# The boundary between images: x in 128 + 64 channels, a convolution by halves of rows, and a new order of the chains

## The chip, the cores and the metric

The kernel runs on one core of one Trainium2 chip. The metric is the device time of one execution in microseconds, the median of three runs. Everything is float32. The five engines are named as the profile names them: PE (TensorE matmul) with PEld (its weight loads), DVE (VectorE), ACT (ScalarE), POOL (GpSimd) and SP (SyncE, which here issues the transfers).

## The reference

Eight images of 64 x 64 tokens with 192 channels pass through two layers, each `x + layer(groupnorm(x))`. Layer 0 is a state-space block with an MLP; the change doesn't touch it. Layer 1 is a scan of each image in four directions (16 states, 384 inner channels). Cut to what matters here:

```python
x = x + _L1_conv_ref(_gn(x), ...)

xz = einsum('bhwc,dc->bhwd', x, in_proj_w)          # 192 -> 2 x 384
xc, z = split(xz, 2, axis=-1)
xc = silu(conv3x3_depthwise(xc) + conv_b)           # 384 channels, 64 x 64
xs = stack of xc by rows, by columns, and both reversed
x_dbl = einsum('bkdl,kcd->bkcl', xs, x_proj_weight) # dt (12), B (16), C (16)
delta = softplus(dts @ dt_projs_weight + bias)
h = exp(delta * A) * h + delta * u * B;  y = sum over n of C * h
y = sum of the four directions (brought back to row order) + xs * Ds
y = (y - mean(y)) * rsqrt(var(y) + 1e-5) * ln_gamma + ln_beta   # over 384
return (y * silu(z)) @ out_proj_w                   # 384 -> 192
```

## The kernel before

Layer 0 runs first over all images and leaves them in eight DRAM tensors `x1s[b]` of 192 channels by 4096 tokens. Layer 1 (`layer1`) then treats one image after another. For each `b` it builds a boundary and then the scan stage.

The scan stage (`main` in `scan`) goes through 32 steps (4 directions, 8 chunks of 512 tokens) of 24 units: two scans on DVE (`run`, L1662), a product with C on POOL (L1676), decays and weighted B on ACT (L1620, L1605), transposes and sums over states on PE (L1646, L1691). Its order is that of the program.

The boundary consists of generators ("chains") whose order `Flow` makes up when the kernel is built: `Flow.run` keeps a planned time for each engine, and takes again and again the chain whose next step can start first, with its rank times 0.01 us added (a chain given later ranks later). Each step names its engine and a planned duration. The order so found is kept on each engine's queue as it is[...].

The chains of `front` prepare image `b`, on tiles of 96 channels by two for the 192 of x:
- `load` (L1133) reads x in tiles of 512 tokens, three times over, once for each block of 128 of the 384 inner channels (`d`);
- `project` (L1148) makes `p_x` with two matmuls over 96 channels each;
- `fill` (L1178) copies it with a bias to a padded image `pad` (66 x 66; two of them);
- `convolve` waits for the whole `pad`: tap 0 on ACT (L1199), eight more on DVE (L1209), each over 4096 tokens;
- `store` and `by_tokens` apply silu (L1222) and store `xo` in three layouts: as it is (L1227), with rows and columns exchanged (`xt`, L1237 and L1241), and by tokens, by way of PE transposes (L1256), copies `xq` on ACT (L1265) and transfers of 256 KB from two buffers (L1268).

The chains of `finish` end image `b - 1`, whose sum `yacc` lies in SBUF: `centre` (mean by matmul, L1288; subtraction, L1296), `square` (L1306), `norm` (L1324, L1325, then the scaling L1331 on DVE and gamma and beta on ACT, L1338), `gate` and `silu` (p_z, L1368, and z, L1386), `product` (L1398), and `project` (p_o, L1415, two matmul groups of 96 output channels; L1424 adds x; L1427 stores). All go by tiles of 512 tokens.

The chain `prologue` starts once all of `front` is stored (`"front"`): it frees front's SBUF space, opens the pools of the scan stage there, loads the first chunk `xc` (L1469), and makes the first `p_d` (L1488), `p_dt` (L1523), `de` (L1536), `duT` (L1552), ten `pw` and two decays. The scan stage's first scan follows once the boundary's work on DVE is through. The last boundary has only `finish`, the first only `front` and the prologue.

The scaled weights (`scaled`, L1107) are made from `wi`, which stays in SBUF for all of layer 1. One PSUM bank (`m1`) belongs to layer 1 as a whole; the boundary has seven, five for `"mm"` and two for `"fx"`.

Of the kernel before, what the change touches and what calls it, by code (L numbers as in the profile page):

```python
# [28 lines left out]
NB1 = TT // 128  # L29
NP1 = N // 2  # L30
# [6 lines left out]
BIG = 60.0  # L37

# [57 lines left out]
class Flow:  # L96
# [48 lines left out]
    def start(self, req, ready):  # L145

        if req[0] == "wait":
            return (-1.0, max(ready, self.at[req[1]])) if req[1] in self.at else None
        if req[0] == "take":
            return (-1.0, max(ready, min(self.slots[req[1]]))) if self.slots[req[1]] else None  # L150
        engine, _, _, after, table = req
        t = max(ready if after is None else after, self.free[engine])
        if engine == "ACT" and table and table != self.table:
            return t + self.TABLE + self.STAY, t + self.TABLE
        return t, t

    def run(self):
        while self.chains:
# [8 lines left out]
            if req[0] == "take":  # L167
# [866 lines left out]
def layer1(tc, consts, x1s, mv1, out, w_in, w_x, w_dt, w_out):  # L1034
# [7 lines left out]
    with ExitStack() as ctx:  # L1042
        pool = lambda name, bufs, **kw: ctx.enter_context(tc.tile_pool(name=name, bufs=bufs, **kw))
        wp = pool("w1", 1)
        sp = pool("s1", 1)
        mp = pool("m1", 1, space=PSUM)
# [5 lines left out]
        wi = wp.tile([CP, CT, 2 * DIN], F32, name="wi1")  # L1052
# [25 lines left out]

        sc, sh = gn_affine(tc, sp, mp, mv1.rearrange("p b t s -> p (b t) s"), grp, eps)
        pb = mp.tile([128, TT], F32, name="p_gb", tag="mm")  # L1080
# [10 lines left out]
        nc.vector.tensor_copy(gb.rearrange("p m b -> p (m b)"), pb[:, : 2 * DT * nb])  # L1091
        keeper = []
# [7 lines left out]
        def scaled(w, b, half):  # L1100

            for ct in range(CT):
                r = yield step(
                    "ACT",
                    0.6,
                    lambda: [
                        nc.scalar.activation(  # L1107
                            w[:, ct],
                            wi[:, ct, half * DIN : half * DIN + DIN],
                            AF.Copy,  # L1110
                            scale=sc[:, b * CT + ct : b * CT + ct + 1],
                        )
                    ],
                )
            return r

        def front(f, cx, mq, b, xo):
# [3 lines left out]
            wx_b = fp.tile([CP, CT, DIN], F32, name="wx1b")  # L1121
            pads = [fp.tile([128, HI + 2, WI + 2], F32, name=f"pad{i}") for i in range(2)]
            for tag, n in (("xl", 2), ("fx", 2), ("pad", 2), ("xs", 2), ("xt", 1), ("xq", 2)):
                f.pool(tag, n)
            got = {}

            def load():
                for d in range(DT):
                    for t in range(NT):
                        tk = slice(t * TT, t * TT + TT)  # L1130
                        yield "take", "xl"
                        xl = got["xl", d, t] = fp.tile([CP, CT, TT], F32, name="xl1", bufs=2)
                        r = yield step("SP", 0.1, lambda: [nc.sync.dma_start(out=xl, in_=image(x1s[b])[:, :, tk])])  # L1133
                        f.at["xl", d, t] = r + 3

            def project():
                yield from scaled(wx_b, b, 0)
                for d in range(DT):
                    for t in range(NT):
                        yield "wait", ("xl", d, t)  # L1140
                        xl = got["xl", d, t]
                        yield "take", "fx"
                        ps = got["ps", d, t] = mq.tile([128, TT], F32, name="p_x1", tag="fx", bufs=2)
                        r = f.at["ps", d, t] = yield step(
                            "PE",
                            1.9,
                            lambda: [
                                nc.tensor.matmul(  # L1148
                                    ps, wx_b[:, ct, d * 128 : d * 128 + 128], xl[:, ct], start=ct == 0, stop=ct == 1
                                )  # L1150
                                for ct in range(CT)
                            ],
                        )
                        f.give("xl", r)

            def fill():
# [11 lines left out]
                for d in range(DT):  # L1168
                    yield "take", "pad"
                    pad = pads[d % 2]  # L1170
                    for t in range(NT):
                        yield "wait", ("ps", d, t)
                        ps = got["ps", d, t]
                        r = yield step(
                            "ACT",
                            0.65,
                            lambda: [
                                nc.scalar.activation(  # L1178
                                    pad[:, 1 + t * RT : 1 + t * RT + RT, 1 : WI + 1],
                                    ps.rearrange("p (h w) -> p h w", w=WI),  # L1180
                                    AF.Identity,
                                    bias=gb[:, d, b : b + 1],
# [3 lines left out]
                        f.give("fx", r)  # L1186
                    f.at["pad", d] = r

            def convolve():
                for d in range(DT):  # L1190
                    yield "wait", ("pad", d)
                    yield "take", "xs"
                    xs = got["xs", d] = fp.tile([128, HI, WI], F32, name="xs1", bufs=2)
                    tap = lambda j: pads[d % 2][:, j // 3 : j // 3 + HI, j % 3 : j % 3 + WI]
                    r = yield step(
                        "ACT",
                        3.7,
                        lambda: [
                            nc.scalar.activation(  # L1199
                                xs, tap(0), AF.Identity, bias=v["kb"][:, d : d + 1], scale=kw[:, d, 0:1]  # L1200
                            )
                        ],
                    )
                    for j in range(1, 9):
                        r = yield step(
                            "DVE",
                            4.4,
                            lambda: [
                                nc.vector.scalar_tensor_tensor(xs, tap(j), kw[:, d, j : j + 1], xs, ALU.mult, ALU.add)  # L1209
                            ],  # L1210
                            r - f.LAG,
                        )
                    f.give("pad", r)
                    f.at["conv", d] = r

            def store():
                for d in range(DT):
                    yield "wait", ("conv", d)
                    xs = got["xs", d]
                    for h in range(2):  # L1220
                        half = xs[:, h * HI // 2 : h * HI // 2 + HI // 2]
                        r = yield step("ACT", 1.9, lambda: [nc.scalar.activation(half, half, AF.Silu)], None, "silu")  # L1222
                        r = yield step(
# [5 lines left out]
                                    in_=half.rearrange("p h w -> p (h w)"),  # L1229
# [3 lines left out]
                        )  # L1233
                        f.fork(by_tokens(d, h, xs, r))
                    yield "take", "xt"
                    xt = fp.tile([128, WI, HI], F32, name="xt1")
# [696 lines left out]
```

## Time and profile before

| what | value |
|---|---|
| median of three runs | 23170.1 us (23146.54 to 23176.63) |
| profiled execution, its time / its span | 23175.73 / 23174.0 us |
| busy PE / DVE / ACT / POOL | 94% / 91% / 87% / 70% of the span |
| granted TensorE clock, mean | 0.971 |
| scan stages, first scan to end of last scan | 2027 to 2031 us, eight times |
| between the last scan of an image and the first of the next | 252.1 to 253.7 us, seven times |

A row of a group gives the line, the engine, the operation, the tile written and those read, the shapes and the count; then the busy time in us and the mean ns of one; then the engine's idle time just before, with what released it. A row of a time line gives the start in us, the time from the first start to the last end, and the operations merged into it, in brackets the idle time before them. A row of the chain of waits gives the start, the length and the piece. The median of the runs lies 5.6 us under the profiled execution.

### The profile page before, as it was taken

To read this page: it belongs to the slowest core of one execution; us is meant where nothing else is said; L and a number is where in the kernel's file an instruction comes from. 1 tells how busy PE (TensorE), PEld (TensorE's weight loads), DVE (VectorE), ACT (ScalarE), POOL (GpSimd) and SP (SyncE) were. 2 spreads that over 40 slices of the span, in tenths; PEclk is the share of its full clock that TensorE was granted. 3 is DMA by queue.
4 is the path that set the end of the run, shared out by engine and by line. 5 is a ranking of instruction groups with operands and counts; after the bars stand their busy time and mean duration, and the time that the engine had idled before them with its cause. 6 is when DMAs were issued, how large, how long until landed. Compare 5 with 4: busy or idle time off the path is not lost.

```text
span 23174.0 us, 348545 instructions
## 1 busy us (share of the span) xinstructions
PE 21762.7 (94%) x118788; PEld 11070.5 (48%) x118788; DVE 21110.3 (91%) x22093; ACT 20048.9 (87%) x35418; POOL 16109.5 (70%) x12872
## 2 busy tenths in 40 slices
PE   8999999979998999899999999999999999999999
PEld 4444444435554555455545544554455445544554
DVE  7888888869998999899989998999899989998998
ACT  5666666759997999799979997999899989988998
POOL 1111111139995999599959995999599869976997
PEclk8999999989999999999999999999999999999999
DMA  1111111133333333333333334333433343333332
GB/s 52 45 44 41 45 45 45 42 96 92 95 93 111 92 92 94 111 94 93 90 114 93 92 87 117 95 92 88 117 92 92 89 117 93 93 91 113 92 94 75
DMA packets 1738653, 1998.38 MB, mean 86 GB/s; under 512 B 537280, under 2 KB 1034848, under 8 KB 1727648
## 3 DMA queue, kind: packets, MB, share of 16 engines
q1 hardware_dynamic: 1736864, 1976.07, 31.9%
q8 instruction: 934, 15.30, 0.3%
q14 instruction: 855, 7.00, 0.1%
HBM read 1360.20 MB, written 212.60 MB: 68 GB/s over the span
## 4 chain that ended last, share of the span: by engine, by line
PE 48%; ACT 22%; DVE 11%; POOL 8%; issue 6%; DMA 3%; SPq 2%; DVEq 0%; POOLq 0%; ACTq 0%
PE g L1646 10%; PE y L1691 10%; ACT ea L1620 10%; ACT pw L1605 9%; POOL hs L1676 7%; DVE hs L1662 3%; PE g L1634 3%; PE p_f L957 3%; DVE xs L1209 3%; PE p_d L1488 2%; PE p_x L450 2%; PE p_f L977 2%; PE p_dt L1523 2%; DMA dr<-de 2%; PE p_o L874 2%
## 5 line engine op out<-in xcount | busy, mean ns | idle before, releaser
L1676 POOL TENSOR_TENSOR hs<-hs,cb 128x1024 f32<-128x1024 f32 x6144 | 14584.3, 2374 | 496.4 <-POOL cy L1674 4.2
L1662 DVE TENSOR_TENSOR_SCAN hs<-ea,cy,g 128x512 f32<-128x512 f32 x10752 | 12894.9, 1258 | 187.2 <-PE g L1646 178.1
L1620 ACT ACTIVATE ea<-dr,an 128x512 f32<-128x512 f32 x12288 | 8139.8, 710 | 528.5 <-DVE hs L1662 507.0
L1605 ACT ACTIVATE pw<-duT,bt 128x384 f32<-128x384 f32 x14336 | 7832.7, 600 | 23.5 <-DVE duT L1552 23.5
L1691 PE MATMUL y<-hs,sel 128*64 128x512 f32 x24576 | 6635.2, 618 | 360.0 <-POOL hs L1676 338.6
L1646 PE MATMUL g<-ident,pw 128*128 128x128 f32 x43008 | 6089.9, 281 | 41.1 <-ACT pw L1605 4.8
L1646 PEld LDWEIGHTS g<-ident,pw 128*128 128x128 f32 x43008 | 4612.5, 141 | 2522.6 <-issue 1254.9
L1674 POOL COPY cy<-hs 128x2 f32<-128x2 f32 x6144 | 1160.7, 189 | 2262.0 <-DVE hs L1662 2228.8
L1634 PEld LDWEIGHTS g<-dg,duT 128*64 128x64 f32 x24576 | 1557.4, 136 | 2053.0 <-issue 1484.6
L1634 PE MATMUL g<-dg,duT 128*64 128x128 f32 x24576 | 2257.9, 282 | 169.4 <-DVE hs L1662 106.1
L1691 PEld LDWEIGHTS y<-hs,sel 128*64 128x64 f32 x24576 | 1234.2, 135 | 1563.0 <-issue 865.6
L1662 DVE TENSOR_TENSOR_SCAN hs<-ea,g 128x512 f32<-128x512 f32 x1536 | 1751.8, 1197 | 129.1 <-PE g L1646 116.8
L367 POOL TENSOR_TENSOR s<-xs 96x512 f32<-96x512 f32 x64 | 121.7, 1902 | 2139.6 <-DVE xs L345 1850.2
L1523 PE MATMUL p_dt<-xdbl,wd 13*128 13x512 f32 x1536 | 857.5, 639 | 96.2 <-DVE duT L1552 71.0
L1209 DVE SCALAR_TENSOR_TENSOR xs<-pad,p,xs 128x4096 f32<-128x4096 f32 x192 | 860.9, 4484 | 50.7 <-ACT xs L1199 43.5
L367 POOL TENSOR_TENSOR s<-sq 96x512 f32<-96x512 f32 x128 | 180.1, 1407 | 942.7 <-ACT sq L380 864.4
L1488 PE MATMUL p_d<-xc,wx 128*44 128x512 f32 x1536 | 788.6, 596 | 19.9 <-DMA xc<-xo 19.9
L957 PE MATMUL p_f<-h,wf 96*128 96x512 f32 x1536 | 762.4, 635 | 44.1 <-ACT zs L552 27.5
L345 DVE SCALAR_TENSOR_TENSOR x<-xx,p,x 96x512 f32<-96x512 f32 x1024 | 784.8, 816 | 15.2 <-ACT x L334 15.0
L345 DVE SCALAR_TENSOR_TENSOR xs<-xin,p,xs 96x512 f32<-96x512 f32 x1024 | 746.1, 768 | 3.6 <-ACT xs L334 3.6
L977 PE MATMUL p_f<-m,wf 128*96 128x512 f32 x1536 | 696.1, 604 | 0.0
L1545 PEld LDWEIGHTS p_du<-ident,de 128*128 128x128 f32 x3072 | 323.9, 141 | 610.1 <-DVE de L1536 406.3
(205 smaller groups left out, 19972.1 us busy)
## 6 DMA issues: line engine op xcount, KB each, us to landing
cb<-cd SPq DMA_DIRECT2D x4096, 128.0 KB
dr<-de SPq DMA_DIRECT2D x3072, 128.0 KB
xc<-xo SPq DMA_DIRECT2D x256, 768.0 KB
dg<-dz SPq DMA_DIRECT2D x256, 512.0 KB
e<-csd SPq DMA_DIRECT2D x256, 384.0 KB
xl<-x SPq DMA_DIRECT2D x256, 384.0 KB
ut<-xo SPq DMA_DIRECT2D x128, 768.0 KB
ut<-xo SPq DMA_DIRECT2D x256, 384.0 KB
```

The source lines that it names most:

```text
L345: nc.vector.scalar_tensor_tensor(im(out[:, ct]), tap(ct, j), w[:, ct, j : j + 1], im(out[:, ct]), ALU.mult, ALU.add)
L957: nc.tensor.matmul(ps, wf1[:, ct, mt * 128 : mt * 128 + 128], h[:, ct], start=ct == 0, stop=ct == 1)
L1209: nc.vector.scalar_tensor_tensor(xs, tap(j), kw[:, d, j : j + 1], xs, ALU.mult, ALU.add)
L1488: nc.tensor.matmul(st["p_d"][:44], wx[:, d, k], st["xc"][:, d], start=d == 0, stop=d == DT - 1)
L1523: nc.tensor.matmul(ps, st["wd"][32:45, d * 128 : d * 128 + 128], xds[s % 2][32:45], start=True, stop=True)
L1605: nc.scalar.activation(st["pw", p, j][:, :, i], st["duT"][:, j].rearrange("p (g c) -> p g c", c=64), AF.Copy, scale=st["bt"][:, j, n : n + 1],
L1620: nc.scalar.activation(ea[:, f], state[s]["dr", d][:, f], AF.Exp, scale=an[:, k, p, at : at + 1])
L1634: nc.tensor.matmul(gs[f][i * 64 : i * 64 + 64, j * 128 : j * 128 + 128], state[s]["duT"][:, j, (2 * d + f) * 64 : (2 * d + f) * 64 + 64], ...
L1646: nc.tensor.transpose(gs[f][:, j * 128 : j * 128 + 128], state[s]["pw", p, j][:, 2 * d + f].rearrange("p a b -> p (a b)"), ident,)
L1662: nc.vector.tensor_tensor_scan(rev(h[:, f]), rev(ea[:, f]), rev(g[f]), 0.0 if first(s) else state[s - 1]["cy"][:, p, d, f : f + 1], ALU.mu ...
L1676: o(nc.gpsimd.tensor_mul(h, h, bc(st["cb", p], 1, [128, 2, TT])))
L1691: o(nc.tensor.matmul(y[half[f]], sel, hc[:, f], start=p == ORDER[0] and k > 0, stop=p == ORDER[-1]))
```

## The change

- **x in 128 + 64 channels.** x is read in pairs of tiles: `xa` has channels 0 to 127 of both tiles, `xb` the other 64, those of the first tile on partitions 0 to 63 and those of the second on 64 to 127. `from_pair` makes both tiles' p_x or p_z with four matmuls. `front` reads an image once and holds it for all three blocks. The output projection writes 128 channels of each tile, and the last 64 of both to the two halves of one bank (`p_o2`).
- **Weights.** `scaled` reads its half of the weights from DRAM for each image and scales it in place; `wi` lies in `yacc`'s space and is used once. The scales are brought to the new partitions by four small transfers at the start of the layer.
- **Convolution by halves.** Each `pad` is convolved in two halves of 32 rows, the first once three of the four pairs are filled (`begin`: tap 0; `convolve`: the others). silu, stores and transposes follow by halves; `xq` holds 1024 tokens, and its transfer 512 KB.
- **Normalisation.** gamma goes into the scaling, which becomes three operations per tile on DVE; beta goes into the product, an operation per pair and block. The ACT operations of L1338 go.
- **Prologue.** x, pads and weights are in one pool (`fr1`), the rest of front in another (`fq1`). Once the last half is convolved and the first halves are stored (`"seed"`), the space of the first is freed and the prologue goes up to `bt` and `duT` there; only pools `pw1`, `bc1` and `e1` wait for `"front"`.
- **Order.** Chains have ranks by name (`RANKS`), those of `finish` grow by 8 per pair (`drift`), and `finish` is listed ahead of `front`. The subtraction, the scaling and the output addition are forked off. PSUM is one pool of eight banks in the boundary; `m1` is opened in `main`.

```diff
+RANKS = dict(
+    begin=-31, fill=-131, enter=-89, load=-44, store=-81, convolve=-1, prologue=-61, project=-11, product=-20, norm=-22,
+    square=-24, silu=-131, centre=-36, gate=-94, weights=285, drift=8,
+)
...
+        def pair_of(xa, xb, src, g, out=False):
+            tk = slice(g * GT, g * GT + GT)
+            moves = [(xa, src[:C1, tk].rearrange("p (i l) -> p i l", i=2))]
+            for i in range(2):
+                at = g * GT + i * TT
+                moves.append((xb[i * C2 : i * C2 + C2], src[C1:, at : at + TT]))
...
+        def from_pair(ps, wa, wb, xa, xb, m):
+            return [nc.tensor.matmul(ps[i], wa[:, m], xa[:, i], start=True, stop=False) for i in range(2)] + [
+                nc.tensor.matmul(
+                    ps[i], wb[i * C2 : i * C2 + C2, m], xb[i * C2 : i * C2 + C2], start=False, stop=True
+                )
+                for i in range(2)
+            ]
...
+            def begin():
+                for d in range(DT):
+                    for h in range(2):
+                        yield "wait", ("pad", d, 2 if h == 0 else 3)
...
             def convolve():
                 for d in range(DT):
-                    yield "wait", ("pad", d)
...
-                    for j in range(1, 9):
-                        r = yield step(
-                            "DVE",
-                            4.4,
...
+                    for h in range(2):
+                        yield "wait", ("begun", d, h)
+                        xs, r = got["xs", d, h], f.at["begun", d, h]
+                        for j in range(1, 9):
+                            r = yield step(
+                                "DVE",
+                                2.24,
...
+            def scale(t, yv, rs, r):
+                for d in range(DT):
...
+                            nc.vector.scalar_tensor_tensor(
+                                yv[:, d], yv[:, d], v["gam"][:, d : d + 1], rs, ALU.mult, ALU.mult
+                            )
...
+                                nc.vector.scalar_tensor_tensor(yv, yv, v["bet"][:, d : d + 1], z, ALU.add, ALU.mult)
...
+                            lambda: [
+                                nc.tensor.matmul(
+                                    ps[i * C2 : i * C2 + C2],
+                                    wo[:, d, C1:],
+                                    yacc[:, d, tk(2 * g + i)],
+                                    start=d == 0,
+                                    stop=d == DT - 1,
+                                )
+                                for d in range(DT)
+                                for i in range(2)
+                            ],
...
-            def prologue(f, mq, front_pools):
-                yield "wait", "front"
-                front_pools.close()
-                for name, n in (("pr1", 2), ("dr1", 4), ("pw1", 8), ("bc1", 3), ("e1", 3)):
+            def prologue(f, mq, cx_b, cx_a):
+                yield "wait", ("conv", DT - 1, 1)
+                yield "wait", "seed"
+                cx_b.close()
+                for name, n in (("pr1", 2), ("dr1", 4)):
...
+                yield "wait", "front"
+                cx_a.close()
+                for name, n in (("pw1", 8), ("bc1", 3), ("e1", 3)):
+                    spool(name, n)
```

## The prediction

> **What bounds it now.** I read the busy slices first, then windows cut at the boundaries between images, then the time lines of VectorE and TensorE in one boundary, then the groups.
>
> The scans of L1662 split the span. Layer 0 ends near 4816 us. Each of the eight images then has a scan stage of some 2030 us, with a boundary before it, and a last boundary closes the run. The change leaves the scan stage alone but for the pool that one PSUM bank comes from, so I price the boundaries. Between the scans of two images:
>
> ```profile
> 4816.00:5023.00 207.00, 108.59 (x259) 52.11 (x259) 116.87 (x50) 89.96 (x86) 3.07 (x8) 0.64 0.52 166
> 13900.00:14153.00 253.00, 215.02 (x531) 92.29 (x532) 165.84 (x77) 152.47 (x166) 6.33 (x9) 0.88 0.47 148
> 23034.00:23174.00 140.00, 129.75 (x300) 53.06 (x300) 55.15 (x44) 64.09 (x79) 5.61 (x5) 0.97 0.16 45
> ```
>
> The columns are window and length, busy time of PE, PEld, DVE, ACT and POOL, granted clock, DMA share, GB/s. The first row is the boundary ahead of image 0, the second that between images 3 and 4 (all seven inner ones are 252 to 254), the third the end. An inner boundary keeps PE busy 215 of 252.6 us and DVE 166. Neither is full, so the order inside decides:
>
> ```profile
> 13951.03 36.21 DVE L1209 SCALAR_TENSOR_TENSOR xs<-pad,p,xs 128x4096 f32<-128x4096 f32 x8 [1.14 <-ACT xs L1199]
> ...
> 14033.45 36.12 DVE L1209 SCALAR_TENSOR_TENSOR xs<-pad,p,xs 128x4096 f32<-128x4096 f32 x8
> ...
> 14100.33 6.12 DMA xc<-xo
> ...
> 14138.50 13.54 PE p_o L1415 x24
> ...
> 14152.67 2.32 DVE L1662 TENSOR_TENSOR_SCAN hs<-ea,g 128x512 f32<-128x512 f32 x2
> ```
>
> (Start, length; the transfer and p_o are from the chain of waits, the rest from VectorE's time line.) The last scan ended at 13900.1. The convolution starts 51 us later, since its first 128 channels need all eight p_x tiles and PE alternates them with the means of the previous image. It runs 118.5 us, 108 of them its own. The tail is 83 us: 31 until all stores have left and xc may be loaded, 6 for that load, 20 to du, 5 for the first pw, and 20 in which PE still projects the previous image. So 252.6 = 51 + 118.5 + 83.
>
> **TensorE.** A matmul with 512 columns shows as two entries, 0.43 us apart at full clock (four p_x entries take 1.72). Now p_x, p_z, p_o and the two means have 96 entries each per inner boundary, 384 x 0.43 = 165 us. Afterwards a pair of tiles takes two matmuls over 128 channels and two over 64, the latter on rows 0-63 and 64-127. If these two run side by side, that is 6 entries in time for 8: p_x and p_z fall to 72 each. p_o has two outputs of 128 columns and one bank in halves of 64: also 72. Means stay at 96. That is 312 x 0.43 = 134 us, 31 less.
>
> Side by side? The trace has column halves (y of L1691 starts its two halves 7 ns apart) and one case of row groups:
>
> ```profile
> 14114.05 0.23 PE L1510 MATMUL p_b<-ident,xdbl 16*128 16x16 f32 x1
> 14114.06 0.69 PE L1523 MATMUL p_dt<-xdbl,wd 13*128 13x512 f32 x1
> ```
>
> p_b reads partitions 0-15, p_dt 32-44, and p_dt starts while p_b runs. I take full overlap; the other end is none, 0.86 us more for each of 24 pairs (21 us).
>
> **A rule against it:** the Trainium skill (TensorEngine Tiling (Array Packing), Key Properties) says that changing the tiling mode drains the array. The row: the p_z before that p_b started at 14113.526, its 0.43 ended at 14113.953, p_b began at 14114.047: 0.09 us lost, and as much from p_dt back to p_o. Two switches per pair are 0.18 x 28 = 5 us. A rule without a price would make the gain uncertain; the row leaves 26 us of it. With transposes (96 x 0.11) and the prologue's matmuls PE's work is some 156 us at full clock, against 182 now.
>
> **VectorE** gets more work. L1209 takes 4.484 us for 4096 elements, and the same operation (L499) 0.739 for 512:
>
> ```profile
> L1209 DVE SCALAR_TENSOR_TENSOR xs<-pad,p,xs 128x4096 f32<-128x4096 f32 x192 | 860.9, 4484 | 50.7 <-ACT xs L1199 43.5
> L499 DVE SCALAR_TENSOR_TENSOR cv<-cin,p,cv 128x512 f32<-128x512 f32 x576 | 406.0, 739 | 10.0 <-ACT cv L484 9.8
> L1338 ACT ACTIVATE yacc<-yacc,p 128x512 f32<-128x512 f32 x192 | 149.8, 804 | 38.5 <-DVE yacc L1331 38.5
> ```
>
> That is 1.045 ns per element, so a half of 2048 takes 0.739 + 1.60 = 2.34, and 2.37 with the 0.03 between dependent ones (now 4.513 start to start). 48 x 2.37 = 114 against 24 x 4.513 = 108: +6. The scale by rs becomes 24 short operations (0.66 to 0.74) for 8 of 1.67: +4. The product becomes 12 of 1.19 to 1.27 for 8 of 1.67: +1.5. Output adds are 12 for 16 of 0.61: -2.5. DVE goes from 166 to about 175 us. ScalarE loses L1338 (24 x 0.8 = 19 us per boundary), and with two pairs of token tiles per half also most of its 20 us of waiting for xo<-xq, since the halves lie 19 us apart. It is at 134 us and hides behind DVE; so do SP's issues (12 loads of x for 24, but 24 of the previous image's loads and stores for 16, and six of weights in place of copies of wi: 2 more in all, at 0.35 us). Without that cover a pair of tiles costs its 1.1 us of issue. The new wait for the weights has nothing behind it on ScalarE before 13913, when the first square starts; p_x waits with it.
>
> **The new inner boundary.** PE is free from the scans at 13907.6. SP's first load leaves now at 13905.3, held by the space of the scan's tiles. Four pairs of three transfers at 0.35 us are out by 13910, and 768 KB take up to 6 us (the xc row). PE then needs three p_x pairs (8.3 us) and two means (5.2): 13921. Two fills (0.69) and tap 0 of a half (1.9) follow: the convolution starts near 13924.5, in 24.5 us for 51. This is where most comes from: three of four pairs now suffice, and p_x ranks ahead of the means.
>
> Of the previous image's DVE work (53 us), 5 is done by then. By the ranks, scale, product and output of the last pair and the output of the third stand behind the convolution (drift 8 per pair), about 12 us. The other 36 lies between the taps: 13924.5 + 114 + 36 = 14075.
>
> The tail: the load of xc goes out with the last tap, since what it reads was stored one half (19 us) earlier. Boundary 0 has this chain undisturbed: load at 4997.4, first scan at 5023.2, 25.8 us. The first pw sits where xs, xt and xq lay, so it waits for their last stores: silu with its table load, xt and four copies take 9 us, then 3 MB at the 237 GB/s that the end of this boundary shows, 13 us. This costs between 0 and 9 us on the chain; I take 5, so 31. The 12 us of DVE work and its matmuls lie inside. 14075 + 31 = 14106, with 2 us of gaps 208 us for 252.6: **-44.5, seven times -311**.
>
> **Boundary 0** has no previous image. The four transfers of scales stand ahead of x on SP (1.4 us), but PE is held by p_gb until 4827.5 in any case: p_x starts at 4828.5 as now, one pair at half clock (5.3) and two at full (5.5), fills and tap 0: convolution at 4844 for 4859.8 (-16); 114 for 111.8 (+2); tail 31 for 51.6 (-20.6). **-34.**
>
> **The end** is PE alone, unbroken from 23041.7 to 23169: 288 entries become 240 (-20.6), switches +3, and the last pair's product and three projections end later by some 4. **-14.**
>
> The sum is -360 on the span of 23174.0. That run took 23175.7, the median of three is 23170.1: 22,810.
>
> **Rivals.**
> - **Clock (B).** The skill (TensorE: Matmul & The Clock Gate, Part 1) has an idle window of about 3.4 us halve the clock. The rows agree: 0.97 where PE never stops, 0.88 inside, 0.64 in boundary 0 with its idle PE. By the full-clock rows PE's 156 us never decides; by the rule, a PE with more gaps may be granted 0.75: 156/0.75 + 7.6 ahead + 8 behind = 224, -243 in all: 22,930. Against it: a PE that becomes the bound is busy and gets its clock back.
> - **Better (C).** The convolution starts after 22 us, the tail is 26, last outputs hide fully: 195 us, -57.5 x 7 - 55: 22,715. For it: DVE's 175 us plus 20.
> - **The row groups do not overlap (D).** PE has 177 us, at 0.88 201 + 16 = 217; the end gains 4: 22,900. The p_b row speaks against it.
> - **Slower (E).** The clock of rival B goes lower, as boundary 0 has it over its last 87 us (0.50 to 0.53). PE decides above the present time from a mean of 0.64 down (156/0.643 + 16 = 259, where seven losses eat the other gains). At 0.60: 276 us, +23 x 7 - 48: 23,285. Against it the same as against B.
>
> **Chances.** Forecast 0.61, B 0.14, C 0.15, D 0.03, E 0.04, no change 0.03 (a wait in an order that I misread holding the convolution back as now). The forecast's own range, from the tail's 0 to 9 us, 5 us of start, and 2 us of taps and gaps, is some 8 us per inner boundary either way: 22,750 to 22,870. 22,695 to 22,965 takes in B, C and D. A difference under 0.2% (46 us) could not be told from none: faster 0.93, same 0.03, slower 0.04.
>
> **What would show it.** The first tap's successor to L1209 some 25 us after the last scan, 48 per boundary of 2.34 us; the two 64-row matmuls starting together; no L1338; xc loaded within 2 us of the last tap; inner boundaries near 208, DVE busy 175 in them; clock above 0.8. It is wrong if the taps still start after 40 us, if the tail stays above 45, or if the scan stages leave 2031 us.

## The result and the profile after

| | before | after |
|---|---|---|
| median, same chip | 23158.32 us (4 runs) | 22852.61 us (4 runs: 22831.2 to 22865.56) |
| ratio | 1 | 0.9867, 95% interval 0.985 to 0.9884 |
| span of the profiled execution | 23174.0 | 22838.4 |
| TensorE clock, mean | 0.971 | 0.976 |

The forecast was 22,810, a gain of 360; the medians are 306 apart, and 22,853 lies inside the forecast's own range of 22,750 to 22,870. Windows of the changed kernel's trace, cut at the same events as before (window and length, busy time of PE, PEld, DVE, ACT and POOL, clock, DMA share, GB/s): the boundary ahead of image 0, one between images, the end; then the inner one in its three parts.

```profile
4787.00:4959.00 172.00, 76.68 (x260) 42.23 (x261) 122.26 (x75) 89.17 (x93) 3.29 (x8) 0.67 0.52 164
11475.20:11690.90 215.70, 182.87 (x536) 71.84 (x536) 169.05 (x116) 133.90 (x146) 6.25 (x9) 0.92 0.44 142
22715.00:22838.00 123.00, 115.24 (x300) 43.43 (x300) 55.34 (x60) 47.34 (x57) 5.62 (x5) 0.97 0.19 55
...
11475.00:11508.00 33.00, 25.61 (x57) 8.25 (x58) 5.83 (x7) 7.36 (x9) 6.45 (x9) 0.84 0.61 155
11508.00:11661.00 153.00, 135.54 (x396) 53.83 (x394) 147.04 (x87) 106.49 (x111) 0.00 (x0) 0.96 0.34 116
11661.00:11691.00 30.00, 21.72 (x84) 9.76 (x84) 16.47 (x25) 20.13 (x28) 0.00 (x0) 0.83 0.81 261
```

Without layer 0, the two profiles differ as follows (us; the three parts before are those of the boundary between images 3 and 4, those after are means):

| piece | before | forecast | after |
|---|---|---|---|
| inner boundary (mean of seven) | 252.6 | 208 | 214.8 (212.1 to 218.9) |
| of it: start to first tap | 51 | 24.5 | 33.4 |
| taps with what lies between | 118.5 | 150.5 | 151.9 |
| tail to the first scan | 83 | 31 (and 2 of gaps) | 29.5 |
| boundary 0 (from layer 0's end to the first scan) | 206.9 | -34 | -35.1 |
| end | 139.8 | -14 | -16.6 |
| eight scan stages | 16242.7 | no change | +10.0 |

The sum is 7 x (214.8 - 252.6) - 35.1 - 16.6 + 10.0 = -306. The two spans lie 336 apart, since layer 0, which the change doesn't touch, ended 29 us earlier in the profile of the changed kernel; in other profiles of this work it ended anywhere from 4787 to 4822.

The taps on VectorE's time line, the first ten of the boundary and its last nine, with the first scan behind them; then the first weighted B and the first wait of the scan stage on ScalarE's; then the page's group:

```profile
11507.93 23.79 DVE L1257 SCALAR_TENSOR_TENSOR xs<-pad,p,xs 128x2048 f32<-128x2048 f32 x10 [15.89 <-ACT xs L1241]
...
11640.03 21.33 DVE L1257 SCALAR_TENSOR_TENSOR xs<-pad,p,xs 128x2048 f32<-128x2048 f32 x9
...
11690.90 4.55 DVE L1784 TENSOR_TENSOR_SCAN hs<-ea,g 128x512 f32<-128x512 f32 x4 [2.63 <-DMA xo<-xq]
```
```profile
11683.35 5.17 ACT L1727 ACTIVATE pw<-duT,bt 128x384 f32<-128x384 f32 x10 [2.08 <-DVE duT L1674]
...
11695.99 1.53 ACT L1742 ACTIVATE ea<-dr,an 128x512 f32<-128x512 f32 x2 [3.73 <-DMA dr<-de]
```
```profile
L1257 DVE SCALAR_TENSOR_TENSOR xs<-pad,p,xs 128x2048 f32<-128x2048 f32 x384 | 900.1, 2349 | 150.2 <-ACT xs L1241 141.3
```

A tap of half an image takes 2.349 us (forecast 2.34) and 2.38 from start to start. The previous image's work now lies between the taps, so that the last nine run alone. pw is released by duT and not by stores. What failed is the start. TensorE's time line there; then the waits of SyncE's queue from 11462 to 11484 (engine and line, what it waited for, us in total, times, longest) and the first load behind them:

```profile
11490.86 1.95 PE L1150 MATMUL p_x<-xa,wxa 128*128 128x512 f32 x4 [0.61 <-DMA xa<-x]
11492.75 1.13 PE L1151 MATMUL p_x<-xb,wxb 64*128 64x512 f32 x4
11496.96 3.57 PE L1150 MATMUL p_x<-xa,wxa 128*128 128x512 f32 x4 [3.08 <-DMA xa<-x]
11500.46 1.19 PE L1151 MATMUL p_x<-xb,wxb 64*128 64x512 f32 x4
...
11503.49 1.13 PE L1151 MATMUL p_x<-xb,wxb 64*128 64x512 f32 x4
```
```profile
SPq L1146 <- PE y L1813: 17.5, 1, 17.5
```
```profile
11482.93 0.34 SPq L1146 DMA_DIRECT2D xa<-x  x1
```

The last scan ended at 11475.19. The first load in SyncE's queue is of the previous image (for p_z, which isn't due for 30 us). It stands there for 17.5 us, until TensorE's last sums of the scan stage (y, L1813) are made, and the new image's loads stand behind it; e1, below, shows that these had nothing of their own to wait for. A second pair of the previous image goes out between the first two of the new one, so that six pairs of 768 KB share the DMA engines for some 20 us. TensorE makes one pair, waits 3.08 us for the second, runs the 128-row matmuls of that one at half clock (3.57 us for 1.98), and the third of the three that the first tap needs ends at 11504.6.

The forecast took its time for the first load of x from the profile of before. Of the two rows there, the one that it used, at 13905.3, is of the previous image (L1353); a first load of x (L1133) had left 22 us earlier, ahead of the last scan's end at 13900.1:

```profile
13883.69 0.58 SPq L1133 DMA_DIRECT2D xl<-x  x1
13905.27 0.31 SPq L1353 DMA_DIRECT2D xl<-x  x1
```

### The profile page after: what moved, and what is told of

Its sections match the earlier page's. It is cut to its first block, busy times and chain, and to the rows that moved or that the text cites. A ratio compares the mean times of both kernels' runs of the same rounds, so it can differ in the third digit from the quotient of the medians.

```text
span 22838.4 us, 348211 instructions
## 1 busy us (share of the span) xinstructions
PE 21469.6 (94%) x118788; PEld 10895.2 (48%) x118788; DVE 21138.2 (93%) x22413; ACT 19918.9 (87%) x35288; POOL 16095.4 (70%) x12872
## 4 chain that ended last, share of the span: by engine, by line
PE 47%; ACT 24%; DVE 10%; POOL 8%; issue 5%; DMA 4%; SPq 2%; DVEq 0%; POOLq 0%; ACTq 0%
ACT ea L1742 11%; ACT pw L1727 10%; PE y L1813 10%; PE g L1768 10%; POOL hs L1798 7%; DVE hs L1784 3%; PE g L1756 3%; PE p_f L970 3%; PE p_d L1610 2%; PE p_x L463 2%; PE p_f L990 2%; DMA dr<-de 2%; PE p_dt L1645 2%; PE p_o L887 2%; PE p_y L804 1%
## 5 line engine op out<-in xcount | busy, mean ns | idle before, releaser
L1742 ACT ACTIVATE ea<-dr,an 128x512 f32<-128x512 f32 x12288 | 8140.7, 710 | 431.2 <-DVE hs L1784 399.8
L1813 PE MATMUL y<-hs,sel 128*64 128x512 f32 x24576 | 6632.6, 618 | 357.5 <-POOL hs L1798 338.2
L1813 PEld LDWEIGHTS y<-hs,sel 128*64 128x64 f32 x24576 | 1234.2, 135 | 1559.2 <-issue 869.4
L1257 DVE SCALAR_TENSOR_TENSOR xs<-pad,p,xs 128x2048 f32<-128x2048 f32 x384 | 900.1, 2349 | 150.2 <-ACT xs L1241 141.3
```

Source lines behind the costliest of these rows:

```text
L1742: nc.scalar.activation(ea[:, f], state[s]["dr", d][:, f], AF.Exp, scale=an[:, k, p, at : at + 1])
L1813: o(nc.tensor.matmul(y[half[f]], sel, hc[:, f], start=p == ORDER[0] and k > 0, stop=p == ORDER[-1]))
```

## The experiments

Where two kernels are compared that didn't run beside each other, the ratios to before are compared; each interval is about 0.0015 to either side, some 35 us. The order of a boundary is planned from the steps' durations, so an edit that alters a step (not one within a step) moves others too.

**The changed kernel itself (e0), and x first (e1).** e0 is unchanged.

> The changed kernel once more, beside the others on one chip. My theory: seven inner boundaries of 212 to 219 us (33 to the first tap, 152 of taps, 30 of tail), 172 ahead of image 0, 123 at the end; total 22850 +- 25 us, ratio 0.986 to 0.989. If layer 0 ended 29 us earlier in the first profile by chance, its end moves again here by some 10 to 30 us.

```diff
-            return [(gen, RANKS[gen.__name__]) for gen in gens]
+            return [(gen, 200 if gen.__name__ == "load" else RANKS[gen.__name__]) for gen in gens]
```

> One number: the previous image's load of x ranks behind the next image's on SP. My theory (SP's queue stands at that load until the scan stage's tiles are free, and x waits behind it and then shares the transfers with it): x lands before PE is free, PE's 3.1 us gap and its half clock go, the first tap comes 26 to 28 us after the last scan for 33.4; boundary 206 to 210 for 215, total -35 to -55 us against the changed kernel. Rival (x's own space is freed only by the last scans, so the order on SP is idle): first tap at 33 as before, total within 10 us.

e0 took 22851.53 (22849.99 to 22853.53), ratio 0.9866; its inner boundaries had a mean of 213.0. e1 took 22823.68 (22817.89 to 22832.74): -28 beside e0, with the first tap after 25.6 to 27.2 us, much as expected. The first load of x on SyncE's time line in the same boundary, whose last scan ended at 11493.08:

```profile
11483.33 0.58 SPq L1146 DMA_DIRECT2D xa<-x  x1
```

x leaves 9.8 us ahead of the last scan's end, where in the changed kernel it left 9.3 us behind it (11484.45, after the pair of the previous image): only its place in the queue had held it. The total fell short of the expected -35: the inner boundary lost 6.3 us at the start and got more than half of it back in taps (151 to 156) and tail, for a mean of 210.2.

**x and its projection first (e1b).** As e1, and the planner is told that x and front's weights are there when their load is issued, so that p_x stands ahead of most means on TensorE's queue.

```diff
-                    f.at["xl", g] = r + 3
+                    f.at["xl", g] = r
...
-            r += 3
+            r += 3 if half else 0
```

> As the run before, and the planner is told that the front's weights and x have landed when issued, which puts p_x ahead of all means but one. My theory: one mean (2.7) and three p_x pairs (9) from 7.6 us after the last scan, fills and tap 0 3.4: first tap at 22 to 24 us, and as VectorE is the bound from there to the end of the taps, the whole of it counts: boundary 203 to 206, total -65 to -85 us against the changed kernel. Rival (PE or ScalarE bounds the taps' stretch, and an earlier start only spreads it): first tap at 23 us, but taps 160 for 152, total within 25 us.

22773.49 us, ratio 0.983 (0.9813 to 0.9846): -78 beside e0. First tap after 22.4 to 24.5 us, inner boundary 205.7. TensorE's time line of the same boundary (last scan's end 11482.59):

```profile
11492.80 1.88 PE L1150 MATMUL p_x<-xa,wxa 128*128 128x512 f32 x4
11494.61 1.13 PE L1151 MATMUL p_x<-xb,wxb 64*128 64x512 f32 x4
11495.67 1.98 PE L1150 MATMUL p_x<-xa,wxa 128*128 128x512 f32 x4
```

The pairs follow each other without a wait, at full clock, and a single mean stands ahead of them where the forecast had two. So the order of the loads and of the first matmuls was the missing part of the forecast: with the loads alone mended (e1), the first tap comes after 26.7 us for the 24.5 forecast, with both (e1b) after 23.8.

**A boundary in the old order (e4).** The new layout, halves and prologue, with the chains' ranks by their place in the list and no drift.

```diff
             if req[0] == "rank":
-                self.rank = req[1]
+                pass
...
-            chains = []
+            chains, ends = [], []
             if b:
-                chains += finish(f, fi_x, mq, b - 1)
+                ends = finish(f, fi_x, mq, b - 1)
...
-            for gen, rank in chains:
-                f.chain(gen, rank)
+            for gen, _ in chains + ends:
+                f.chain(gen)
```

> The changed kernel with all its new instructions and spaces, but with the chains' order of before: each chain's rank is its place in the list, the front's chains ahead of the finish's, and the requests for a rank that drifts from pair to pair do nothing. Theory (of the 38 us that an inner boundary won, the larger part is the new layout and halves; the order is there so that the finish fills gaps without holding the taps up): start of the convolution about 25 to 30 us (the front's load of x now goes ahead of the finish's), taps 151 to 160, tail longer because the finish's work is left over: 35 to 60 us; boundary 215 to 240, so 0 to +175 us against the changed kernel. Rival (the order carries most of the gain): boundary over 240, +175 us and more. Second rival (only the load's place counts): the time of the kernel with the front's load ahead, 22775 to 22825.

Ratio 0.9936 (0.9921 to 0.9951), 0.0070 or 162 us above the changed kernel. Inner boundaries take 236 to 240 us (mean 237.0). Windows of one of them, taps and tail:

```profile
11587.20:11713.20 126.00, 85.83 (x247) 37.37 (x246) 124.32 (x60) 79.76 (x79) 0.00 (x0) 0.82 0.37 130
11713.20:11793.20 80.00, 70.26 (x211) 25.78 (x209) 37.87 (x48) 40.73 (x57) 0.00 (x0) 0.94 0.42 132
```

The taps run nearly alone, 126 us instead of 151, and the previous image's work comes after them: the tail is 80 us, with TensorE busy for 70. The expected taps and tail were both wrong; the total lies within the expectation, and the rival's bound of 240 is just missed in the mean. Of 252.6 - 213.0 = 39.6 us, layout, halves and prologue gave 15.6 without the order, and the order 24 on top of them. How the 15.6 divide isn't shown: no run undoes the halves or the single load of x alone.

**A late prologue (e3).**

```diff
                 yield "wait", ("conv", DT - 1, 1)
+                yield "wait", "front"
                 yield "wait", "seed"
```

> The changed kernel, but the prologue of the next image's first tile of time waits until the last of the forward tokens and copies is stored, as before the change, instead of only for the convolution's last half: nothing of the prologue lies beside the tail of the stores. Theory (the prologue in the space of x is what shortened the tail from 83 to 30 us, together with the halves): the tail grows by 10 to 20 us in each of the 8 boundaries ahead of an image, 80 to 160 us in all; start and taps stay as they are (33 and 151 us). Rival (the tail is set by the stores of the last half and their landing; the prologue's place is free): the tail grows by under 4 us, under 30 us in all.

Ratio 0.9901 (0.9884 to 0.9917), 81 us above the changed kernel. Start and taps are unchanged (31 to 35 and 151 to 154), the tail is 42.6 for 28.4 in e0: TensorE's p_d waits 6.14 us for xc, whose load is issued after the last xq's store. Boundaries cost 7 x 14.3 + 17.6 = 118 more, but the scan stages 36 less, 4.5 each. The theory holds, at the lower end of its range. Of the 14 us of tail, then, nearly a third comes back in the scan stage behind it.

**gamma and beta back on ScalarE (e5).** The scaling is one `tensor_mul` of 1536 elements by rs on VectorE again, gamma and beta an `activation` per block, the product a plain multiplication.

```diff
+                r = yield step("DVE", 1.7, lambda: [nc.vector.tensor_mul(yv, yv, bc(rs, 1, full))], r - f.LAG)
+                f.give("rs", r)
                 for d in range(DT):
                     r = yield step(
-                        "DVE",
-                        0.62,
+                        "ACT",
+                        0.75,
                         lambda: [
-                            nc.vector.scalar_tensor_tensor(
-                                yv[:, d], yv[:, d], v["gam"][:, d : d + 1], rs, ALU.mult, ALU.mult
+                            nc.scalar.activation(
+                                yv[:, d],
+                                yv[:, d],
+                                AF.Identity,
+                                bias=v["bet"][:, d : d + 1],
+                                scale=v["gam"][:, d : d + 1],
                             )
...
-                                nc.vector.scalar_tensor_tensor(yv, yv, v["bet"][:, d : d + 1], z, ALU.add, ALU.mult)
+                                nc.vector.tensor_mul(yv, yv, z)
```

> The changed kernel, but the normalisation's scaling as before: one tensor multiplication of 1536 elements by the inverse deviation on VectorE, gamma and beta back on ScalarE as one pass of 512 elements each, and the gate's product as a plain multiplication of two tensors. Theory (VectorE with its taps sets the end of the boundary; ScalarE has room): VectorE's busy time falls or rises by under 4 us a boundary (three passes of 0.62 become one of 1.7, the product goes from 1.15 to about 1.1 each), ScalarE gains 24 passes x 0.75 = 18 us; the time moves by -25 to +25 us in all. Rival (ScalarE's evictions of the next pad and its stores are what the taps wait for): plus 5 to 15 us a boundary, 40 to 120 us.

Ratio 0.9893 (0.9878 to 0.9908), some 62 us above the changed kernel. VectorE is 3 us less busy (166.12) and ScalarE 20 more (152.17), as counted. But the rival has only the sum right, not the place: the taps got shorter (146 to 150 us). The chain of the previous image became longer by a pass on ScalarE, and more of it fell behind the last tap: in one boundary the tail is 43 us, with TensorE busy for 38.8 of them (25.8 of 29.8 in e0).

**Scaling and product on GpSimd (e6).** On e1b, with gamma and beta on ScalarE as in e5, and:

```diff
+                r = yield step("POOL", 3.6, lambda: [nc.gpsimd.tensor_mul(yv, yv, bc(rs, 1, full))], r)
...
+                        q = yield step("POOL", 2.4, lambda: [nc.gpsimd.tensor_mul(yv, yv, z)])
```

> The version with x's loads and the first projection first (e1b), and besides it the finish's scaling and its gating product on GpSimd as plain multiplications, gamma and beta on ScalarE: 32 us of VectorE's 169 us of a boundary go to an engine that is idle there, ScalarE gains some 18 us. Theory (in the stretch of the taps, VectorE is the bound: taps of 2.35 us spaced at 2.38 within a half): VectorE busy 135 to 140 us, the inner boundary falls from 206 to 180 to 195 us, with the clock of TensorE or the finish's end as the next bound; 75 to 200 us less than e1b in all. Rival (the taps aren't the bound, TensorE at a clock of 0.9 or the tail is; or GpSimd's passes slow VectorE's[...]): no change against e1b within 25 us, or slower, with taps of over 2.45 us.

Ratio 0.9894 (0.9879 to 0.9909): 0.0064 or some 150 us above e1b. The groups of the tap stretch, first e1b's taps, then e6's, then GpSimd's own in e6's whole boundary; then one tap and the GpSimd pass beside it, from the two time lines:

```profile
L1257 DVE SCALAR_TENSOR_TENSOR xs<-pad,p,xs 128x2048 f32<-128x2048 f32 x48 | 112.4, 2348 | 11.3 <-ACT xs L1241 10.2
```
```profile
L1257 DVE SCALAR_TENSOR_TENSOR xs<-pad,p,xs 128x2048 f32<-128x2048 f32 x48 | 134.6, 2811 | 11.5 <-ACT xs L1241 10.2
```
```profile
L1498 POOL TENSOR_TENSOR yacc<-yacc,z 128x1024 f32<-128x1024 f32 x12 | 39.1, 3278 | 24.0 <-ACT yacc L1425 24.0
L1418 POOL TENSOR_TENSOR yacc<-yacc,yrs 128x1536 f32<-128x1536 f32 x8 | 35.0, 4384 | 109.2 <-ACT yrs L1409 84.9 <-DVE xa L1541 24.3
```
```profile
11618.48 3.87 DVE L1257 SCALAR_TENSOR_TENSOR xs<-pad,p,xs 128x2048 f32<-128x2048 f32 x1
```
```profile
11614.71 5.49 POOL L1418 TENSOR_TENSOR yacc<-yacc,yrs 128x1536 f32<-128x1536 f32 x1 [3.89 <-ACT yrs L1409]
```

The same 48 taps take 22 us more, of the 32 that VectorE was spared. In this boundary 33 of them have no GpSimd pass beside them and take 2.35 us each; the other 15 take 3.83 on average and up to 5.50. The passes grow too: the first kind (L1418) takes up to 5.49 us beside taps and 3.45 behind the last one. That is the second half of the rival: the Trainium skill (SBUF — State Buffer, Who interferes with whom) says that a VectorE instruction with two inputs in SBUF contends with a GpSimd one that reads SBUF, and a tap is one. The stretch of the taps thus stays at 151 us (154 in e1b), and the 150 us are lost behind it: the slower chain of the previous image ends in a tail of 47 us for 28.

**Pairs without side by side (e2).** The four matmuls of a pair in the order 128, 64, 128, 64 rows.

```diff
-            return [nc.tensor.matmul(ps[i], wa[:, m], xa[:, i], start=True, stop=False) for i in range(2)] + [
-                nc.tensor.matmul(
-                    ps[i], wb[i * C2 : i * C2 + C2, m], xb[i * C2 : i * C2 + C2], start=False, stop=True
-                )
-                for i in range(2)
-            ]
+            out = []
+            for i in range(2):
+                out.append(nc.tensor.matmul(ps[i], wa[:, m], xa[:, i], start=True, stop=False))
+                out.append(
+                    nc.tensor.matmul(
+                        ps[i], wb[i * C2 : i * C2 + C2, m], xb[i * C2 : i * C2 + C2], start=False, stop=True
+                    )
+                )
+            return out
```

> The four matmuls of a pair in the order 128 rows, 64 rows, 128 rows, 64 rows: the same work, but no two on different row groups side by side. My theory (inside a boundary VectorE is the bound once the taps run): a pair takes 1.0 to 1.3 us more on PE, 24 of them 24 to 31 us per inner boundary, of which 3 to 4 us show at the first tap and 0 to 4 later; the end stage 12 to 15 longer; total +35 to +75 us. Rival (the change gains by fewer PE passes): each inner boundary 24 to 31 us longer, total +180 to +230 us, two thirds of the gain gone.

23383.33 us, ratio 1.0092 (1.0075 to 1.0109): 532 above e0, over twice what the larger expectation had. Five of the inner boundaries take 270 to 286 us, two 244. A row of TensorE's time line in one of the five, and a window in it:

```profile
11650.16 2.05 PE L1152 MATMUL p_x<-xa,wxa 128*128 128x512 f32 x2 [2.96 <-DMA xa<-x]
```
```profile
11675.00:11738.00 63.00, 63.00 (x64) 15.48 (x62) 23.43 (x10) 20.68 (x18) 0.00 (x0) 0.50 0.04 17
```

After the wait of 2.96 us each matmul, of 128 rows or 64, takes 2.0 us, and for 63 us TensorE is busy without a break at a clock of 0.50. So the run does not price the side-by-side rows by themselves. The next runs ask why the clock stays low.

**Full rows (e7b), beside e1b once more (e8).** The 64-channel weights lie in zeroed tiles of 128 rows, so that each matmul reads all 128 rows of `xb` and nothing switches; two gate buffers instead of three make room.

```diff
-                    ps[i], wb[i * C2 : i * C2 + C2, m], xb[i * C2 : i * C2 + C2], start=False, stop=True
+                    ps[i], wb[:, i, m], xb, start=False, stop=True
```

> The version with x's loads and the first projection ahead (e1b) once more, as the base of the two kernels that run beside it. Both theories: inner boundaries of 204 to 208 us, first tap 22 to 25 us, ratio to before 0.981 to 0.985.

> The base (e8) with the 64-channel part of each projection from x as a 128-row matmul: the weights of the 64 channels in the rows of their tile, zeros in the other 64 rows, x's 128 rows as they lie. No row groups, no change of rows; 16 passes of 512 columns a pair instead of the time of 12, in the same order of matmuls. To make room, two gate buffers instead of three; both weights are cleared by GpSimd and loaded half by half. Theory (the alternation of 128 and 64 rows is what kept the clock at 0.50 in the serial version, and passes alone cost little here): the clock of inner boundaries stays at 0.9 and above, a pair takes 3.40 to 3.45 us at full clock, TensorE 10 to 12 us more a boundary, the boundary +2 to +8 us, +15 to +65 us in all. Rival (a longer gap-free TensorE is enough for the low clock): a stretch of over 50 us at 0.50 in most boundaries, +300 us and more. Second rival (passes are the gain): +80 to +100 us.

e8 took 22764.69 (ratio 0.9828, 0.9812 to 0.9845), e7b 22821.76 (0.9853): +57. Inner boundaries take 211.8 for e8's 205.5. Boundary 0 takes 12 more: with the step that clears the weights, the planned order has their loads behind those of x, and the first p_x comes at 4825.38 for e8's 4813.64. One of e7b's inner boundaries:

```profile
11488.08:11699.25 211.17, 187.43 (x527) 82.35 (x528) 169.09 (x116) 141.35 (x151) 7.58 (x11) 0.95 0.42 134
```

A pair takes 3.43 us and TensorE is busier, yet at a clock of 0.95, where e8 has 0.92. More passes alone do not cost the clock. The 6.3 us are also a rough upper bound on what the side-by-side rows are worth in an inner boundary, since they hold more than the passes: two means instead of one now stand ahead of the first p_x, and one gate buffer is gone.

**Fewer changes of rows (e7).** On e1b, every second pair begins with its 64-row matmuls.

```diff
+            return [one(i) for one in ((short, tall) if turn else (tall, short)) for i in range(2)]
```

> The base (e8) with one thing changed: of the pairs of tiles that TensorE projects from x, every second one begins with its two 64-row matmuls and ends with its two 128-row ones, so that two pairs in a row change their rows once instead of three times between them. 24 pairs a boundary, so up to 24 changes of about 0.2 us less, where the pairs follow each other and no transposition or other matmul stands between. Theory (TensorE doesn't set the end of the taps; only ahead of the first tap do pairs follow each other): TensorE 2 to 4 us less a boundary, the time 0 to 15 us less in all. Rival (TensorE's busy time is on the path): 20 to 40 us less in all.

TensorE's time line ahead of the first tap:

```profile
11492.14 1.99 PE L1160 MATMUL p_x<-xb,wxb 64*128 64x512 f32 x8
11494.05 3.70 PE L1156 MATMUL p_x<-xa,wxa 128*128 128x512 f32 x8
11497.68 1.99 PE L1160 MATMUL p_x<-xb,wxb 64*128 64x512 f32 x8
```

Two pairs now take 5.54 us (11492.14 to 11497.68), 2.77 each for 2.97: half the changes are gone, and each was worth 0.2 us. The time is 22780.35, 16 above e8 and not below. The rival's 20 to 40 us did not come; a gain of a few us, as the theory allows, is too small to be told apart here.

**Serial pairs with x there in time (e9).** e2's order on e1b.

> The version with x and the first projection ahead (e1b), with the four matmuls of a pair in the order 128, 64, 128, 64 rows (as e2), so that no two 64-row matmuls stand together. In e2 TensorE waited 3 us for x just ahead of the first pair and then ran at half clock; here x is there before TensorE comes to it. At full clock a pair takes 4.2 us for 2.97, 24 x 1.25 = 30 us more of TensorE a boundary. Theory (the alternation does not bring the clock down, it only fails to raise it once it is down): the pairs ahead of the first tap run at full clock, inner boundaries of 212 to 230 us, +50 to +190 us against e1b. Rival (the alternation brings the clock down by itself): the pairs start at full clock and fall to half within some 10 us in most boundaries, inner boundaries over 240, +300 us and more.

23182.3 us, ratio 1.0004 (0.9995 to 1.0013): about 400 above e1b. By its size this is the rival; the trace shows the theory. TensorE's time line in a boundary, and two windows:

```profile
9367.45 1.02 PE L1152 MATMUL p_x<-xa,wxa 128*128 128x512 f32 x2
...
9422.71 1.13 PE L1152 MATMUL p_z<-xa,wza 128*128 128x512 f32 x2 [1.65 <-ACT yrs L1411]
...
9425.37 2.07 PE L1152 MATMUL p_z<-xa,wza 128*128 128x512 f32 x2 [0.46 <-ACT z L1480]
9427.38 2.07 PE L1154 MATMUL p_z<-xb,wzb 64*128 64x512 f32 x2
...
9449.41 4.13 PE L1369 MATMUL p_m<-yacc,on 128*128 128x512 f32 x6
```
```profile
9400.00:9420.00 20.00, 20.00 (x42) 6.48 (x41) 9.95 (x5) 9.62 (x8) 0.00 (x0) 1.00 0.13 52
9420.00:9440.00 20.00, 17.89 (x22) 4.82 (x22) 16.55 (x10) 7.88 (x10) 0.00 (x0) 0.62 0.00 0
```

From 9367 to 9413 the alternating matmuls run at full clock, 1.05 us each. Two waits of 1.65 and 0.46 us follow, the clock halves, and the alternating matmuls then stay at half clock, until matmuls of 128 rows alone (p_m) bring it back at 9452. It is so in all 24 stretches of over 20 us at half clock in the inner boundaries of e2 and e9: TensorE has waited 1.65 us or more just ahead, the alternating matmuls run at half clock to their end, and the clock is back 2.4 to 5.2 us after matmuls of 128 rows alone have begun. So the alternation does not bring the clock down; it does not bring it back up. What does bring it down stays open in part, since the same wait at the same place leaves it at full in the next boundary:

```profile
11706.00 1.13 PE L1152 MATMUL p_z<-xa,wza 128*128 128x512 f32 x2 [1.65 <-ACT yrs L1411]
```

The theory's size failed because the pairs do not stay free of waits: in the boundary shown first those of p_z meet two, and inner boundaries take 242 to 266 us.

## Why the prediction was right, and where it was wrong

- **The start was mis-sized: 24.5 us forecast, 33.4 measured.** The step read "four pairs of three transfers at 0.35 us are out by 13910, and 768 KB take up to 6 us". Its first load, "held by the space of the scan's tiles", was one of the previous image, and so are two of the six pairs: x could have left ahead of the last scan (e1), but stood in the queue behind the first of them and shared the DMA engines with both. The step priced one pair's transfer instead. 7 x 8.9 = 62 us is more than the whole miss of 54. e1, which alters only the order of the loads, takes 6.3 of the 8.9 us away and 28 us of the time; e1b, with p_x ahead of a mean besides, 78 us.
- **Taps with what lies between: right**, 151.9 for 150.5, though VectorE's total is 169 and not 175. By their groups the taps add 4.9 us, scaling 2.6, product 1.3 and output additions -2.6, for the +6, +4, +1.5 and -2.5 forecast; the total, which counts overlapping durations once, rises by 3.
- **The tail: right in the sum**, 29.5 for 31. The 5 us for stores on the way to pw came to nothing, since pw was released by duT; the load of xc took 8.3 us for 6. e3 shows that the early prologue is worth 14 us of it.
- **The row groups: right** that they run side by side (both 64-row matmuls' four entries take 1.13 us). A change of rows costs 0.2 us, not 0.09, so a pair takes 2.97 for the forecast 2.76. By e7 this is not where time went.
- **Boundary 0 and end: right**, -35.1 and -16.6 for -34 and -14. In boundary 0 two misses cancelled: the start took 33.8 us (some 27.6 forecast), the tail 21.5.
- **Scan stages: 10 us more.** The prediction named a stage beyond 2031 us as a sign of being wrong, and three of the eight take 2033. Nearly all of the difference arises within the first 12 of a stage's 1536 scans, and the rest run as before. At the start of one of the three, ScalarE waits 3.73 us for dr (L1742 at 11695.99), where the stage ahead of it, of 2030.8 us, has no such wait.
- **The rivals.** The clock (B, E) did not fall here, 0.92 for 0.88, but e2 and e9 show that this danger was real, and that it hung on the order of four matmuls. "No overlap" (D) was priced at 217 us a boundary; e7b, with the passes of no overlap and no changes of rows, gives 211.8 on the better base. Two sums of the rivals are off: from their terms B comes to about -250 and not -243, and D to some 22,885 and not 22,900.
- **The range held in part by luck.** It allowed 5 us for the start, which missed by 8.9; taps, tail and the 2 us of gaps, each within 2 us of the forecast, left the boundary 6.8 us above it, inside the 8 us allowed.

The fastest version is that of e1b, 0.983 and 0.9828 in its two runs (e1b, e8), some 80 us below the changed kernel.

## What to carry to other kernels

When transfers are moved forward, write out the whole queue at that moment: what stands at its head and waits for what, whose transfer goes first, how many bytes share the DMA engines. One transfer's duration says little. Work of another chain that fills the gaps of a critical chain on an engine can be worth more than fewer passes: here the order gave 24 us a boundary, all the rest 16, and in e7b full rows cost no more than some 6. Before work is handed to GpSimd, look at what VectorE does at that moment.

## What the hardware showed

- At half clock, serial alternation of 128- and 64-row matmuls left TensorE at 0.50 although it was busy for 63 of 63 us (e2); at full clock the same sequence kept 1.00 for 46 us (e9). The Trainium skill (TensorE: Matmul & The Clock Gate, Part 1) has about 3.4 us of sustained activity bring the full clock; here it did not. With the two 64-row matmuls side by side, or with zeros in full rows, it did: no half clock in an inner boundary of e1b or e7b lasts longer than 10.3 us. Whether the changes of rows or the idle half of the rows is behind it stays open. Nor did the clock need the idle window of about 3.4 us that the prediction took from the same page: it fell within a microsecond of a wait of 1.65 us in some boundaries of e2 and e9, and in others the same wait left it at full.
- A change between 128-row and 64-row matmuls costs about 0.2 us of TensorE: a pair takes 2.97 us with two changes and 2.77 with one (e1b, e7).
- SyncE's queue stands at its first transfer: one that waited 17.5 us held others behind it that had nothing to wait for (the changed kernel, e1).
- A tap on VectorE takes 2.35 us alone and 3.83 on average with a GpSimd pass beside it; over the 48 of a boundary the mean is 2.81 (e6).
